# Layer 0 of a four-layer hybrid network: norm and batch statistics moved off VectorE, B replicated in fp32, TensorE's queue reordered

## The chip, the cores and the metric

The kernel runs on one core of one Trainium2 chip, in one launch. The metric is the device time of that core in microseconds. A core has five engines with queues of their own, which the tables below call PE (TensorE), DVE (VectorE), ACT (ScalarE), POOL (GpSimd) and SP (SyncE, which here only starts DMAs). PEld is the loading of TensorE's weights. Each engine takes its instructions in the order in which the program gives them; semaphores make one wait for another.

## The reference, cut to what matters

The input x is 4 images of 96 channels on 64 x 64 points, so 4 sequences of 4096 tokens. Layer 0 is two Mamba blocks, then a 1x1 fusion with a global-pool branch and a batch norm:

```python
mu = seq.mean(-1); var = ((seq - mu) ** 2).mean(-1)
h = (seq - mu) * rsqrt(var + EPS) * ln_g + ln_b          # over the 96 channels
xs, z = split(h @ in_w, 2)
xc = silu(causal conv of 4 taps of xs + conv_b)           # 192 channels
dt, Bm, Cm = split(xc @ xproj_w)                          # 6, 16, 16 columns
delta = softplus(dt @ dt_w + dt_b)
dA = exp(delta * A); dBx = delta * Bm * xc                # 192 x 16 states
hstates[l] = dA[l] * hstates[l-1] + dBx[l]                # along the tokens
y = (sum over states of hstates * Cm + Dp * xc) * silu(z)
seq = seq + y @ out_w                                     # twice (two blocks)
out = fus_w @ [seq, relu(mean(x) @ gp_w)] + fus_b
out = (out - mean) * rsqrt(var + EPS) * bn_g + bn_b + x   # over images and points
```

Layers 1 to 3 (a convolution block, two attention-like blocks with quantised feed-forward parts) come after it, and the change doesn't touch them.

## The kernel before, in words

Layer 0 works through 32 **items** (`items`): 4 stretches s of T = 1024 tokens, times 2 blocks i, times 4 images b. An item has 192 channels x 16 states = 3072 rows, which are 24 **tiles** of 128 rows (32 channels x 4 states) by 1024 tokens. `order` gives the tiles: p picks 64 of the channels, j one half of them, g one of four groups of 4 states. Of the 24 tiles, 8 are "POOL tiles" (`pool_tiles`).

For each tile, `rep` (line 438) spreads 4 rows of B over 128 partitions with a product on PE into PSUM (one replica serves the one or two tiles of a group, nine replicas an item); `exp` (line 447) makes dA on ACT; `scan` (line 464) multiplies delta*xc with the replica on DVE (line 471) and runs the recurrence on DVE (line 475); `times_c` (line 481) multiplies the states with C on POOL; `sum_y` (line 500) sums over states on PE. For a POOL tile the product with B is made on POOL instead (`times_b`, line 461), and ACT writes dA to PSUM (`dap`).

[...] The pool `l0x` holds two buffers of two banks, shared in turn by the replica x, the product u and dap; `l0p` holds two buffers `ps` of one bank, used by every other product; `l0y` holds two for y.

What comes before the tiles of an item is `first_stage` (line 251): load x, centre it, take the norm's scale, multiply, then the products for xc, B, C, dt, delta and z, and the stores of delta and delta*xc to DRAM, from where they are read back spread over partitions. Its steps are hung on **slots** by hand: `at_slot(t)` puts a step beside tile t of the item before. After the tiles come `gate` (line 511, DVE), `project` (line 518) and `finish` (line 527 or 529), the last at slot 17 of the next item, and `keep_stats` (line 537), the batch norm's statistics with `bn_stats` on DVE.

The loop over m at the end of `layer0` sets the order: at each tile it issues the scan, then the next replica (or the exp of the next POOL tile), the exp three tiles ahead, `times_c` of the tile before, then `sum_y` and its like, then the steps hung on this slot. The order is exactly that of the program (`manual_schedule`), so what stands ahead in a queue holds up what is behind it.

In the kernel before, the norm runs so: PE centres (line 274) with the channels on partitions, ACT squares and copies (280, 281), PE sums the squares over channels with a matrix of ones (287), ACT makes the scale as exp(-0.5 ln(.)) (292, 293), DVE multiplies (299). POOL keeps the three last columns for the next stretch (`halo`, lines 268, 301). B is replicated in bf16: ACT casts it three times to bf16, each time what the parts before left over (lines 335, 347), PE subtracts the parts (line 342), and the replica sums the three parts (line 195).

Of the kernel before, what the change touches and what calls it, by code (L numbers as in the profile page):

```python
# [50 lines left out]
class Net:  # L51
# [20 lines left out]
    def consts(self, ctx):  # L72
        tc, nc, ins = self.tc, self.nc, self.ins
        pool = ctx.enter_context(tc.tile_pool(name="const", bufs=1))
        self.cpool = pool
        self.vec = pool.tile([C, NV96], F32, name="vec")
        nc.sync.dma_start(self.vec, ins["vec96"])
        self.vec128 = pool.tile([128, NV128], F32, name="vec128")
        nc.sync.dma_start(self.vec128, ins["vec128"])
        self.ones = pool.tile([C, C], F32, name="ones")  # L80
        nc.vector.memset(self.ones, 1.0)
        self.eps = pool.tile([128, 1], F32, name="eps")
        nc.vector.memset(self.eps, EPS)
        self.ident = pool.tile([128, 128], F32, name="ident")
        make_identity(nc, self.ident)
        self.center = pool.tile([C, C], F32, name="center")
        nc.vector.tensor_scalar_add(self.center, self.ident[:C, :C], -1.0 / C)
        self.stats = pool.tile([C, NT // MB, 6], F32, name="stats")
        self.osc = pool.tile([C, 1], F32, name="osc")
        self.osh = pool.tile([C, 1], F32, name="osh")  # L90


    def layer0(self, dram, scratch):
        tc, nc, ins = self.tc, self.nc, self.ins
        x_in = ins["x"]
        with ExitStack() as ctx:
            cp = ctx.enter_context(tc.tile_pool(name="l0c", bufs=1))
            psum = ctx.enter_context(tc.tile_pool(name="l0p", bufs=2, space=PSUM))
            psum_x = ctx.enter_context(tc.tile_pool(name="l0x", bufs=2, space=PSUM))
# [16 lines left out]
            sel_b = cp.tile([C, 4, 128], BF16, name="sel_bq")  # L116
            part = cp.tile([C, 2, C], BF16, name="partq")
            fo = cp.tile([128, 3, C], F32, name="fo")
            dp = cp.tile([128, 2, 3, 128], F32, name="dp")
            sel_r = load(cp, "sel_r", [128, 32])  # L120
            xproj = load(cp, "xproj", [128, 3, 2, 3 * 2 * NST + DTR])
# [7 lines left out]
            fbias = cp.tile([C, B], F32, name="fbias")  # L129
            pooled = cp.tile([C, B * NSC], F32, name="pooled")  # L130

            with tc.tile_pool(name="l0s", bufs=1) as wk:
# [30 lines left out]
                nc.vector.tensor_copy(sel_b, load(wk, "sel_b", [C, 4, 128]))  # L163
                nc.vector.tensor_copy(part, load(wk, "part", [C, 2, C]))
# [14 lines left out]
            dbl = cp.tile([97 + DTR, T], F32, name="dbl")  # L179
            nc.vector.memset(dbl[C:], 1.0)  # L180
            r3s = [cp.tile([C, T], BF16, name=f"r3{k}") for k in range(2)]
            for r3 in r3s:
                nc.vector.memset(r3, 0.0)
# [7 lines left out]

            def mm(ps, w, rhs, start=True, stop=True, shift=0, **kw):
                for at in halves:
                    at_in = slice(at.start + shift, at.stop + shift)
                    nc.tensor.matmul(ps[:, at], w, rhs[:, at_in], start=start, stop=stop, **kw)  # L195
# [54 lines left out]
            def first_stage(k):  # L250
# [11 lines left out]
                @at_slot(-11)  # L262
                def _():
                    m["xn"] = load_x(b, s, i)
                    if s == 0:
                        nc.gpsimd.memset(n[:, :3], 0.0)
                    else:
                        nc.gpsimd.tensor_copy(n[:, :3], halo[:, b, i])

                @at_slot(-7)  # L270
                def _():
                    m["ps"] = [tile_ps(), tile_ps()]
                    for at, ps in zip(halves, m["ps"]):
                        nc.tensor.matmul(ps, self.center, m["xn"][:, at], start=True, stop=True)

                @at_slot(-6)
                def _():
                    m["sq"] = wk.tile([C, T], F32, name="sq", tag="sq")
                    for at, ps in zip(halves, m["ps"]):
                        nc.scalar.activation(m["sq"][:, at], ps, AF.Square)  # L280
                        nc.scalar.copy(n[:C, 3 + at.start : 3 + at.stop], ps)

                @at_slot(-5)
                def _():
                    m["ps"] = [tile_ps(), tile_ps()]
                    for at, ps in zip(halves, m["ps"]):
                        nc.tensor.matmul(ps, self.ones, m["sq"][:, at], start=True, stop=True)

                @at_slot(-4)
                def _():  # L290
                    for ps in m["ps"]:
                        nc.scalar.activation(ps, ps, AF.Ln, scale=1.0 / C, bias=self.eps[:C])
                        nc.scalar.activation(ps, ps, AF.Exp, scale=-0.5)

                @at_slot(-3)
                def _():
                    for at, ps in zip(halves, m["ps"]):
                        x = n[:C, 3 + at.start : 3 + at.stop]
                        nc.vector.tensor_mul(x, x, ps)  # L299
                    if s < NSC - 1:  # L300
                        nc.gpsimd.tensor_copy(halo[:, b, i], n[:, T:])
# [14 lines left out]
                parts_of("xc", [(w_x[:, i, k], k) for k in range(4)], n, ((-2, 0), (-1, 1), (1, 3)), 2)  # L316

                @at_slot(3)
                def _():
                    nc.scalar.activation(m["xc"], m["xc"], AF.Silu)  # L320
                    exp_set()

                nb = 6 * NST + DTR
                r3 = m["r3"] = r3s[k % 2]

                @at_slot(5)
                def _():
                    m["ps"] = [tile_ps(128), tile_ps(128)]
                    join([ps[:nb] for ps in m["ps"]], xproj[:, :, i], m["xc"])

                @at_slot(6)
                def _():

                    for at, ps in zip(halves, m["ps"]):
                        nc.scalar.copy(r3[:32, at], ps[:32])
                        nc.scalar.copy(dbl[:nb, at], ps[:nb])
                    cd = m["cd"] = dram.tile([2 * NST, T], F32, name="cd", tag="cd", bufs=2)
                    nc.sync.dma_start(cd, dbl[: 2 * NST])

                def less(r):  # L340
                    for at, ps in zip(halves, m["ps"]):
                        nc.tensor.matmul(ps[:C], part[:, r], r3[:, at], start=False, stop=True, skip_group_check=True)

                def next_part(r):
                    rows = slice(32 * r + 32, 32 * r + 64)
                    for at, ps in zip(halves, m["ps"]):
                        nc.scalar.copy(r3[rows, at], ps[rows])

                for r in range(2):
                    at_slot(7 + 2 * r)(lambda r=r: less(r))  # L350
                    at_slot(8 + 2 * r)(lambda r=r: next_part(r))

                parts_of("delta", [(dtw[:, i], 0)], dbl, ((10, 11), (10, 12), (11, 12)), 1)

                @at_slot(12)
                def _():
                    nc.scalar.activation(m["delta"], m["delta"], AF.Softplus)  # L357
                    exp_set()

                parts_of("z", [(w_z[:, i], 3)], n, ((12, 13), (13, 14), (13, 14)), 3)  # L360

                @at_slot(13)
# [18 lines left out]
                @at_slot(19)  # L381
# [56 lines left out]
            def rep(m):  # L438

                k, t = divmod(m, NTL)  # L440
                x = psum_x.tile([128, T], F32, name="rep", tag="xu")
                mm(x, sel_b[:, order[t][1], :], made[k]["r3"])
                u = psum_x.tile([128, T], F32, name="u", tag="xu")
                return x, u

            def exp(m):
# [3 lines left out]
                if on_pool(m):  # L450
                    da = psum_x.tile([128, T], F32, name="dap", tag="xu")
# [11 lines left out]
            def scan(m, x, u):  # L463
# [6 lines left out]
                else:  # L470
                    nc.vector.tensor_mul(u, made[k]["ud", h, j], x)  # L471
# [49 lines left out]
            def finish(k):  # L521
# [3 lines left out]
                for at, ps in zip(halves, made[k]["out"]):  # L525
                    if i == 0:
                        nc.scalar.copy(o[:, at], ps)
                    else:
                        nc.scalar.activation(o[:, at], ps, AF.Identity, bias=fbias[:, b : b + 1])
                a = b * L + s * T  # L530
                nc.sync.dma_start(scratch[:, a : a + T] if i else xd[:, b], o)

            def keep_stats(k):
                b, s, i = items[k]
                a = b * L + s * T
                for at in halves:
                    nc.vector.bn_stats(self.stats[:, (a + at.start) // MB, :], made[k]["x"][:, at])
# [4 lines left out]
            with tc.manual_schedule(engines=engines):  # L542
# [3 lines left out]
                for m in range(first, last + 19):  # L546
                    k, t = divmod(m, NTL)
                    if 0 <= m < last:
                        scan(m, *xu)
                    if 0 <= m + 1 < last:  # L550
                        if on_pool(m + 1):
                            exp(m + 1)
                        elif (t + 1) % NTL in group_starts:
                            xu = rep(m + 1)
# [8 lines left out]
                    for k0 in range(max(k - 1, 0), min(k + 1, len(items))):  # L563
# [15 lines left out]
                        if at == 42 and items[k0][2]:  # L579
                            keep_stats(k0)  # L580
# [8 lines left out]
            nc.vector.bn_aggr(mv, self.stats)  # L589
# [695 lines left out]
def _constants():  # L1285
# [3 lines left out]
    sel_b = np.stack([(k[:, None] % 32 == 4 * g + p[None] // 32) for g in range(4)], 1)  # L1289
    sel_r = (p[:, None] % 32 == p[None, :32]).astype(f32)  # L1290

    part = np.zeros((C, 2, C))
    for r in range(2):
        for q in range(r + 1, 3):
            part[32 * r : 32 * r + 32, r, 32 * q : 32 * q + 32] = -np.eye(32)
# [23 lines left out]
        "part": part.astype(f32),  # L1319
# [102 lines left out]
```

## Time and profile before

The time before is 4220.29 us, the median of three runs (4219.02 to 4225.47). The profiled run took 4222.8 us.

| what | value |
|---|---|
| DVE busy in the whole run | 3189.6 us, 76% |
| POOL busy | 2997.8 us, 71% |
| PE busy | 3233.2 us, 77% |
| ACT busy | 2514.7 us, 60% |
| scans on DVE (L475), all forms | 768, of 2270 to 2348 ns each |
| products with B on DVE (L471) | 512 of 1226 ns |
| products with C on POOL (L481) | 768 of 2359 ns |
| products with B on POOL (L461) | 256 of 2365 ns |
| replicas on PE (L195) | 576 products of 485 ns |

A line of the profile's groups reads: line, engine, operation, what it writes and reads, shapes, count | time busy, mean length of one in ns | idle time of the engine just before them, and what ended that idle time. A line of the timeline gives the start and the length in us, the engine, the line, the operation, the count, and in brackets the idle time before it. One fp32 product shows as two records.

### The profile page before, as it was taken

What the parts mean: (1) busy time and instruction counts of PE and PEld (TensorE: products, weight loads), DVE (VectorE), ACT (ScalarE), POOL (GpSimd) and SP (SyncE); (2) the same over time, 40 slices, a digit from 0 to 9 for tenths busy, and PEclk for the clock granted to TensorE, in tenths of its full rate; (3) what the DMA queues carried; (4) which work ended last, traced back from release to release, by engine and by line L of the source; (5) the groups of instructions that cost most, each with busy time, mean ns of one, the idle gap of its engine ahead of it and who ended that gap; (6) DMA issues with size and microseconds to landing.
All of it is one profiled execution on the core that took longest, in us unless ns stands there. A gap on an engine that the chain in (4) does not pass through costs nothing. (4 is left out here: it accounts for less than half of the span.)

```text
span 4222.8 us, 42511 instructions
## 1 busy us (share of the span) xinstructions
PE 3233.2 (77%) x13088; PEld 1310.8 (31%) x13088; DVE 3189.6 (76%) x2474; ACT 2514.7 (60%) x4098; POOL 2997.8 (71%) x1651
## 2 busy tenths in 40 slices
PE   6677677777767777776777776579999888887987
PEld 2111112111211211121121111277445436555642
DVE  4999999999999999999999999731222583444649
ACT  4666666666666666666666665322555575544547
POOL 1999999999999999999999999611110264333418
PEclk8788888888878888888888887669999998899989
DMA  7557566566656656665665666363000000001111
GB/s 171 136 149 172 132 155 162 139 147 158 164 136 152 161 137 147 161 161 137 151 161 137 147 158 165 77 202 130 0 0 1 1 1 5 23 28 28 44 43 53
DMA packets 183276, 468.02 MB, mean 111 GB/s; under 512 B 53108, under 2 KB 55134, under 8 KB 179968
## 3 DMA queue, kind: packets, MB, share of 16 engines
q1 hardware_dynamic: 183048, 465.31, 43.6%
q8 instruction: 103, 1.69, 0.2%
q14 instruction: 125, 1.02, 0.1%
HBM read 391.62 MB, written 73.50 MB: 110 GB/s over the span
## 5 line engine op out<-in xcount | busy, mean ns | idle before, releaser
L481 POOL TENSOR_TENSOR hs<-hs,crep 128x1024 f32<-128x1024 f32 x768 | 1799.2, 2359 | 108.1 <-DVE hs L475 55.0
L475 DVE TENSOR_TENSOR_SCAN hs<-da,state,u 128x1024 f32<-128x1024 f32 x384 | 901.7, 2348 | 24.9 <-DVE u L471 0.5
L455 ACT ACTIVATE dap<-ddb,nega 128x1024 f32<-128x1024 f32 x256 | 286.3, 1118 | 722.0 <-DVE u L471 721.6
L471 DVE TENSOR_TENSOR u<-udb,rep 128x1024 f32<-128x1024 f32 x512 | 627.7, 1226 | 72.3 <-PE rep L195 40.2
L455 ACT ACTIVATE da<-ddb,nega 128x1024 f32<-128x1024 f32 x512 | 583.7, 1143 | 67.7 <-DVE hs L475 65.7
L195 PE MATMUL rep<-r,sel_bq 96*128 96x512 bf16 x576 | 226.8, 485 | 514.4 <-DVE hs L475 505.9
L461 POOL TENSOR_TENSOR up<-udb,brep 128x1024 f32<-128x1024 f32 x256 | 605.3, 2365 | 4.7 <-DMA ud<-du 4.7
L500 PE MATMUL y<-hs,sel_r 128*32 128x512 f32 x3072 | 501.9, 724 | 4.6 <-POOL hs L481 4.6
L475 DVE TENSOR_TENSOR_SCAN hs<-dap,state,up 128x1024 f32<-128x1024 f32 x192 | 447.1, 2329 | 16.4 <-ACT dap L455 16.4
L205 PE MATMUL ps<-n,w_x 97*64 97x512 f32 x1536 | 424.7, 680 | 10.9 <-DVE n L299 10.8
L475 DVE TENSOR_TENSOR_SCAN hs<-da,u 128x1024 f32<-128x1024 f32 x128 | 293.0, 2289 | 8.1
L195 PEld LDWEIGHTS <-sel_bq 96*128 96x128 bf16 x576 | 39.1, 103 | 780.2 <-DVE hs L475 582.2
L1002 POOL CAST hq<-y 128x512 fp8e5<-128x512 f16 x192 | 118.5, 641 | 222.1 <-DVE y L1001 222.1
L205 PEld LDWEIGHTS ps<-n,w_x 97*64 97x64 f32 x1536 | 152.2, 155 | 287.3 <-issue 217.6
L205 PE MATMUL ps<-n,w_z 97*64 97x512 f32 x384 | 121.1, 714 | 129.3 <-ACT z L309 116.2
L1150 POOL TENSOR_TENSOR av<-av,ec 128x780 f32<-128x780 f32 x32 | 58.8, 1838 | 197.3 <-ACT av L1147 197.3
L796 POOL TENSOR_TENSOR xc<-xc,rs 96x512 f32<-96x512 f32 x32 | 40.4, 1266 | 209.8 <-ACT rs L795 163.8
L500 PEld LDWEIGHTS y<-hs,sel_r 128*32 128x32 f32 x3072 | 65.6, 116 | 319.1 <-issue 167.8
L219 PE MATMUL ps<-xc,xproj 64*102 64x512 f32 x384 | 152.1, 952 | 3.5 <-ACT xc L320 3.5
L475 DVE TENSOR_TENSOR_SCAN hs<-dap,up 128x1024 f32<-128x1024 f32 x64 | 145.3, 2270 | 7.6 <-ACT dap L455 5.7
L373 POOL TENSOR_TENSOR du<-delta,xc 128x512 f32<-128x512 f32 x96 | 122.6, 1277 | 32.1 <-ACT delta L357 22.3
L1147 ACT ACTIVATE av<-xr_ps,vec 128x65 f32<-128x65 f32 x384 | 117.0, 424 | 47.5 <-PE xr_ps L1135 47.5
(255 smaller groups left out, 6067.3 us busy)
## 6 DMA issues: line engine op xcount, KB each, us to landing
ddb<-dd SPq DMA_DIRECT2D x768, 128.0 KB, 3.3
udb<-ud SPq DMA_DIRECT2D x768, 128.0 KB, 4.4
crep<-cd SPq DMA_DIRECT2D x512, 128.0 KB, 4.0
brep<-cd SPq DMA_DIRECT2D x256, 128.0 KB, 3.6
dd<-delta SPq DMA_DIRECT2D x64, 384.0 KB, 3.9
ud<-du SPq DMA_DIRECT2D x192, 128.0 KB, 3.2
band<-in_band SPq DMA_DIRECT2D x24, 1024.0 KB, 4.8
gt<-in_idft SPq DMA_DIRECT2D x64, 256.0 KB, 2.7
```

What stands on the lines that cost most here:

```text
L195: nc.tensor.matmul(ps[:, at], w, rhs[:, at_in], start=start, stop=stop, **kw)
L205: nc.tensor.matmul(ps[rows], w[:, 64 * p : 64 * p + 64], rhs[:, at.start + shift : at.stop + shift], start=k == 0, stop=k == len(ws) - 1, ...
L219: nc.tensor.matmul(ps, w[rows, p], x[rows, p], start=start and p == 0, stop=p == 2)
L373: nc.gpsimd.tensor_mul(u, m["delta"][:, of], m["xc"][:, of])
L455: nc.scalar.activation(da, made[k]["dd", h, j], AF.Exp, scale=nega[:, col : col + 1])
L461: nc.gpsimd.tensor_mul(u, made[k]["ud", h, j], made[k]["brep", g])
L471: nc.vector.tensor_mul(u, made[k]["ud", h, j], x)
L475: nc.vector.tensor_tensor_scan(hs[:, 1:], made[k].pop(("da", t)), u, 0.0 if s == 0 else st, ALU.mult, ALU.add)
L481: nc.gpsimd.tensor_mul(hs[:, :T], hs[:, 1:], made[k]["crep", order[t][1]])
L500: nc.tensor.matmul(made[k]["y", p][row : row + 32], sel_r, made[k]["hs", t][:, at], start=False, stop=True, skip_group_check=True,)
L1002: nc.gpsimd.tensor_copy(q[:, m, :], y2, saturate=False)
L1147: nc.scalar.activation(v[:, k, d], xr[:, at], AF.Identity, scale=self.v128(w, cg + d), bias=self.v128(bias, cg + d))
```

## The change

Four things are done in layer 0:

1. **The norm leaves DVE and goes over tokens on partitions.** PE centres with x as the weights, so that 128 tokens land on partitions and 96 channels lie side by side; ACT squares them and adds up in the same instruction (`accum_out`), makes the scale for 8 x 128 tokens, and multiplies with a scale per partition; PE turns the result back with the identity; ACT copies it to n. The halo copies go from POOL to ACT.
2. **The batch statistics leave DVE.** `finish` adds up its output as it writes it, and a second ACT instruction adds up the squares around a shift (the first half tile's mean).
3. **B is replicated in fp32** straight from dbl, which now has two buffers; the three bf16 parts and their products go. The left half of the tokens is read from rows 0 to 31 and the right half from rows 32 to 63, two copies of B that xproj already makes. The last product with B of a group before a POOL tile is written over its own replica. PSUM's pool has one buffer x, and one that u and dap share, in place of two shared by all three.
4. **PE's steps are moved to other slots**, mostly those behind a replica.

```diff
-            psum_x = ctx.enter_context(tc.tile_pool(name="l0x", bufs=2, space=PSUM))
+            psum_x = ctx.enter_context(tc.tile_pool(name="l0x", bufs=1, space=PSUM))
...
+                @at_slot(-6)
+                    m["ps"] = [tile_ps(128), tile_ps(128)]
+                    for q in range(8):
+                        nc.tensor.matmul(m["ps"][q // 4][:, q % 4 * C : q % 4 * C + C],
+                            m["xn"][:, q * 128 : q * 128 + 128], self.center, start=True, stop=True)
+                @at_slot(-5)
+                    for q in range(8):
+                        nc.scalar.activation(m["nt"][:, q], m["ps"][q // 4][:, q % 4 * C : q % 4 * C + C],
+                            AF.Square, accum_out=m["rs"][:, q : q + 1])
+                    nc.scalar.activation(m["rs"], m["rs"], AF.Ln, scale=1.0 / C, bias=self.eps)
+                    nc.scalar.activation(m["rs"], m["rs"], AF.Exp, scale=-0.5)
+                @at_slot(-4)
+                    for q in range(8):
+                        nc.scalar.mul(m["nt"][:, q], x, m["rs"][:, q : q + 1])
+                @at_slot(-3)
+                    for q in range(8):
+                        nc.tensor.matmul(m["ps"][q // 4][:, q % 4 * 128 : q % 4 * 128 + 128],
+                            m["nt"][:, q], self.ident, start=True, stop=True)
+                @at_slot(-2)
+                        nc.scalar.copy(n[:, :3], halo[:, b, i])
                     for at, ps in zip(halves, m["ps"]):
                         nc.scalar.copy(n[:C, 3 + at.start : 3 + at.stop], ps)
-                        nc.vector.tensor_mul(x, x, ps)
-                        nc.gpsimd.tensor_copy(halo[:, b, i], n[:, T:])
+                        nc.scalar.copy(halo[:, b, i], n[:, T:])
...
-                parts_of("xc", ..., n, ((-2, 0), (-1, 1), (1, 3)), 2)
+                parts_of("xc", ..., n, ((-1, 1), (0, 2), (2, 4)), 2)
-                @at_slot(5)
+                @at_slot(7)
                     join([ps[:nb] for ps in m["ps"]], xproj[:, :, i], m["xc"])
-                        nc.scalar.copy(r3[:32, at], ps[:32])
                         nc.scalar.copy(dbl[:nb, at], ps[:nb])
-                for r in range(2):
-                    at_slot(7 + 2 * r)(lambda r=r: less(r))
-                    at_slot(8 + 2 * r)(lambda r=r: next_part(r))
-                parts_of("delta", ..., ((10, 11), (10, 12), (11, 12)), 1)
+                parts_of("delta", ..., ((9, 10), (9, 10), (10, 11)), 1)
-                parts_of("z", ..., ((12, 13), (13, 14), (13, 14)), 3)
+                parts_of("z", ..., ((11, 12), (12, 13), (13, 14)), 3)
...
-                x = psum_x.tile([128, T], F32, name="rep", tag="xu")
-                mm(x, sel_b[:, order[t][1], :], made[k]["r3"])
-                u = psum_x.tile([128, T], F32, name="u", tag="xu")
+                x = psum_x.tile([128, T], F32, name="rep", tag="x")
+                for q, at in enumerate(halves):
+                    rows = slice(32 * q, 32 * q + 32)
+                    nc.tensor.matmul(x[:, at], sel_b[rows, order[t][1]], made[k]["dbl"][rows, at], start=True, stop=True)
...
+                    u = x if on_pool(m + 1) else psum_x.tile([128, T], F32, name="u", tag="u")
                     nc.vector.tensor_mul(u, made[k]["ud", h, j], x)
...
-                        nc.scalar.activation(o[:, at], ps, AF.Identity, bias=fbias[:, b : b + 1])
+                    nc.scalar.activation(o[:, at], ps, AF.Identity, bias=fbias[:, b : b + 1], accum_out=self.sums[:, a : a + 1])
+                    nc.scalar.activation(ps, ps, AF.Square, bias=sbias[:, b : b + 1], accum_out=self.squares[:, a : a + 1])
-                    nc.vector.bn_stats(self.stats[:, (a + at.start) // MB, :], made[k]["x"][:, at])
```

## The prediction

> **What bounds the kernel now.** I read the page's slices first: VectorE (DVE) and GpSimd (POOL) stand at 9 tenths from slice 2 to slice 26, so layer 0 is where the change acts; the chain of work that ended last shows only later layers. Then the stretches, 500 us each, inside that plateau (columns after the length: PE, PEld, DVE, ACT, POOL busy, granted clock, DMA share, GB/s):
>
> ```profile
> 500.00:1000.00 500.00, 363.96 (x1432) 95.02 (x1428) 476.43 (x283) 334.52 (x515) 476.85 (x226) 0.83 0.62 151
> 1000.00:1500.00 500.00, 363.00 (x1402) 96.00 (x1404) 479.39 (x285) 329.13 (x510) 477.19 (x226) 0.82 0.60 149
> ```
>
> Two engines are busy 95%, and each feeds the other. ACT (66%) and PE (73%) matter only where one of the two waits for them. Next, the groups by shape in 500 to 2500 us:
>
> ```profile
> L481 POOL TENSOR_TENSOR hs<-hs,crep 128x1024 f32<-128x1024 f32 x586 | 1372.4, 2358 | 80.3 <-DVE hs L475 38.0 <-DMA udb<-ud 19.3 <-DMA crep<-cd 10.4
> L475 DVE TENSOR_TENSOR_SCAN hs<-da,state,u 128x1024 f32<-128x1024 f32 x343 | 805.4, 2348 | 22.3 <-DVE u L471 0.5
> L471 DVE TENSOR_TENSOR u<-udb,rep 128x1024 f32<-128x1024 f32 x391 | 479.4, 1226 | 48.0 <-PE rep L195 26.0 <-DMA ud<-du 3.7
> L475 DVE TENSOR_TENSOR_SCAN hs<-dap,state,up 128x1024 f32<-128x1024 f32 x172 | 400.5, 2329 | 15.2 <-ACT dap L455 15.2
> ...
> L299 DVE TENSOR_TENSOR n<-n,ps 96x512 f32<-96x512 f32 x48 | 31.1, 668 | 0.3
> ...
> L537 DVE BATCH_NORM_STATS2 stats<-x 96x6 f32<-96x512 f32 x24 | 15.1, 668 | 0.0
> ...
> L268 POOL COPY n<-halo 97x3 f32<-97x3 f32 x23 | 4.4, 192 | 0.0
> L301 POOL COPY halo<-n 97x3 f32<-97x3 f32 x17 | 3.2, 188 | 14.2 <-DVE n L299 14.2
> ```
>
> The 586 times-C products are 24 per item: 24.4 items in 2000 us, a period of **81.9 us per item**, and 32 items make layer 0. The four stretches from 500 to 2500 sum to 1908.6 us of DVE and 1905.7 of POOL: 78.2 and 78.0 of a period. Of DVE's 3.7 idle us, named waits are 26.0 (replica), 15.2 (dap) and 3.7 us of 2000: 1.8 an item. The other 1.9 are the steps between instructions. POOL idles 3.9, of which 14.2/24.4 = 0.6 is the halo copy waiting for the norm.
>
> Last the timeline of one item, PE alone but for one DVE line (start, length, instructions):
>
> ```profile
> 1004.47 1.03 PE L195 MATMUL rep<-r,sel_bq 96*128 96x512 bf16 x2 [6.49 <-DVE hs L475]
> ...
> 1026.44 1.12 PE L492 MATMUL y<-xc,dp 128*128 128x512 f32 x2
> ...
> 1035.81 1.32 PE L205 MATMUL ps<-n,w_z 97*64 97x512 f32 x4 [3.68 <-ACT z L309]
> ...
> 1038.92 1.03 PE L195 MATMUL rep<-r,sel_bq 96*128 96x512 bf16 x2
> ...
> 1039.99 1.23 DVE L471 TENSOR_TENSOR u<-udb,rep 128x1024 f32<-128x1024 f32 x1 [0.76 <-PE rep L195]
> ...
> 1041.66 2.82 PE L219 MATMUL ps<-z,out_w 64*96 64x512 f32 x12
> ```
>
> A replica is released when the scan before a POOL tile ends, and has that tile's scan (2.33 us) to hide in. It does so unless PE comes late: at 1038.92 it stood behind the z product, which had waited for ACT's copy.
>
> [...] after 6.49 us idle a replica takes 1.03 us, others 0.60. [...] 12 records of z,out_w (two sets of 64 rows) took 2.82 us, 0.43 for each pair; a lone fp32 product needs 0.43 per record (dp: two records in 1.12). No run yet shows sets of 32 rows. [...]
>
> **The change part by part.**
>
> *DVE loses* two norm products (31.1/24.4 = 1.27 us an item) and bn_stats (15.1/24.4 = 0.62): **1.9 us**, all of it in the queue of a 95% engine. It gains one-off small operations only.
>
> *POOL loses* both halo copies, 7.6/24.4 = 0.3, and the 0.6 of waiting behind one: 0.9. A wait for PE's reads remains only for the memset of the first 8 items.
>
> *Replica in fp32.* Nine per item, two products of 32 rows each. If the row sets run together: two steps of 0.43 plus the tail that dp shows (1.12 - 0.86 = 0.26) = 1.12 us warm against 0.60; at half clock two of 0.85 plus about 0.3 = 2.0 against 1.03. Window: 1004.47 to the next product's start at 1006.76 is 2.29. Both fit, the cold one by 0.3. If they run one after the other: 1.98 warm, 3.7 cold; the cold one misses by 1.4. I take together, since the trace shows it for 64 rows at 96 columns, and keep the other for the range. The product over its own replica (line 473 of the changed kernel) costs nothing: DVE still reads and writes PSUM; and dap's own buffer is free after the scan of the tile before last, not after the last product, which can only help the 15.2 us of dap waits.
>
> *TensorE's order.* In the changed program's queue z stands two slots ahead of the replica of slot 15 (one before), xproj stands behind that of slot 7, center behind that of slot 18. The 26.0/24.4 = 1.07 us of replica waits came mainly from two lateness spots per item (0.76 at 1039.99, 0.63 at 1050.19), one behind z and one behind center: both orders are cured. I credit 0.8.
>
> *B without its three bf16 parts.* Four small PE products (4 x 0.38) and six ACT casts (6 x 0.57 = 3.4) go; dbl gets a second buffer. All of it lay beside the scans, so I count nothing; delta comes a slot earlier and its store with it.
>
> *Norm on ACT and PE.* ACT loses squares, copies, Ln, Exp (2 x (0.60 + 0.58 + 0.64 + 0.57) = 4.8) and the 3.4 of casts. It gains 8 squares with a sum, Ln and Exp of 8 columns, 8 scalings, 2 copies (1.16), the halo copies (0.36), and 0.7 for half the items' second batch sum. An ACT copy of 97x96 took 0.24 us (L936); how much a sum adds the trace doesn't show: nothing, or at most a second instruction of 0.24. So the eight squares take 1.9 to 3.9, I take 2.6; the scalings 2.0. Sum 2.6 + 0.5 + 2.0 + 1.2 + 0.4 + 0.7 = 7.4 against 8.2: ACT stays near 66%. But order counts: ACT's exp for the POOL tile of slot 21 is queued behind the squares, and these wait for center. From the replica of slot 18: replica 1.1, y 1.06, eight transposing products at 0.43 (L714, of like shape: 55.2 us busy, 128 products) 3.4, the last four squares and Ln, Exp 1.8, exp 1.1 = 8.5 us; DVE needs it after a POOL scan and two tiles, 2.33 + 2 x 3.6 = 9.5. Hidden by 1; cold PE takes 1 to 3 us more. I charge 0.4 an item.
>
> *POOL nearer its limit:* at 80 us it would idle 2.3, where waits for DMA (29.7/24.4 = 1.2) remain. I charge 0.3 for the coupling.
>
> *Ends:* the first item's norm is longer by some 4 us at half clock, its B parts shorter by 3; the small operations at the end replace bn_aggr (1.0). Nothing.
>
> Sum per item: -1.9 - 0.8 + 0.4 + 0.3 = -2.0; times 32 = -64; **4220 - 64 = 4156 us**.
>
> **The rivals.**
> (a) *Small gain:* POOL is as loaded as DVE, and once DVE is ahead only POOL's 0.9 counts: 32 x 0.9 = 29, 4191. For it: 78.0 against 78.2. Against: much of POOL's idle time (38.0) is waiting for DVE, which a faster DVE shortens.
> (b) *A new wait eats it:* the ACT block or cold replicas hold DVE for 2 us an item, 4220 or a little more; 4222.
> (c) *Row sets in series:* in the timeline of one item four of nine replicas take 1.03 us, so are cold: 4 x 1.4 = 5.6, the warm ones that come late add 1, less 2.7: +3.9 an item, 4345. For it: no set of 32 rows at 128 columns is in the trace. Against: pairs of 64 rows at 102 columns (xproj) do go together.
>
> **How the numbers follow.** Forecast 0.56, (a) 0.20, (b) 0.13, (c) 0.11. If DVE's named waits vanish too, the period is 78.2 + 1.9 - 1.9 = 78.2: -3.7 x 32 = 4102; half-way, 4125, is the low end. The high end takes in (a) and (b): 4228. Outside stay most of (c) and a tail below, 0.14. Faster by over 0.2% (below 4212): 0.56 + 0.20 + a little of (b) = 0.78; same 0.06; slower 0.16.
>
> **What would show it.** Right: period near 80 us; no norm product or bn_stats on DVE; waits of DVE for the replica under 26 us in 2000, replicas of 1.1 (warm) and 2.0 us (cold); POOL over 96% busy. Wrong: replica records that follow each other at 0.43 steps four times; DVE waiting for dap at slot 21 in every item; squares of over 0.5 us; POOL waiting for DMA for 2 us an item, which would leave the period at 81.

## The result and the profile after

The changed kernel takes **4105.66 us** (median of four runs, 4099.68 to 4110.68) against 4222.64 for the kernel before on the same chip: ratio 0.9723, 95% interval [0.9706, 0.974], 117 us faster. The forecast was 4156, with 4125 as its low end: right in direction, too small by almost half.

Read on the two profiled runs (4222.8 and 4106.5 us), the 116.3 us lie here. The scans, from the first one's start to the last one's end, take 2516.2 us in place of 2615.8 (-99.6). The first scan starts at 81.8 in place of 91.1 (-9.3). From the last scan to the batch norm's reciprocal it is 14.7 in place of 16.4 (-1.8). Layers 1 to 3, in which no instruction changed, are 5.6 us shorter; over the 14 profiles of this study that stretch varies from 1488.5 to 1499.4, so this part says nothing.

The stretches of the changed kernel inside layer 0 (columns as before: PE, PEld, DVE, ACT, POOL, clock, DMA share, GB/s):

```profile
1000.00:1500.00 500.00, 412.76 (x1728) 129.63 (x1728) 486.06 (x276) 339.51 (x675) 496.09 (x224) 0.83 0.67 160
1500.00:2000.00 500.00, 410.98 (x1726) 126.32 (x1722) 485.68 (x274) 334.25 (x635) 494.99 (x223) 0.83 0.64 154
```

POOL is now busy 99%, DVE 97%, in place of 95% each. The groups by shape in 500 to 2500 us:

```profile
L484 POOL TENSOR_TENSOR hs<-hs,crep 128x1024 f32<-128x1024 f32 x610 | 1426.2, 2360 | 23.7 <-DVE hs L478 18.5 <-ACT rs L283 1.3 <-PE ps L296 1.2
...
L478 DVE TENSOR_TENSOR_SCAN hs<-da,state,rep 128x1024 f32<-128x1024 f32 x183 | 429.7, 2348 | 15.9
L478 DVE TENSOR_TENSOR_SCAN hs<-dap,state,up 128x1024 f32<-128x1024 f32 x183 | 426.1, 2329 | 5.7 <-ACT dap L456 5.5
...
L442 PE MATMUL rep<-dbl,sel_b 32*128 32x512 f32 x914 | 321.4, 779 | 360.0 <-DVE hs L478 345.1 <-DVE u L474 13.4 <-PE y L503 0.9
...
L474 DVE TENSOR_TENSOR u<-udb,rep 128x1024 f32<-128x1024 f32 x202 | 248.3, 1229 | 26.0 <-PE rep L442 8.7
L474 DVE TENSOR_TENSOR rep<-udb,rep 128x1024 f32<-128x1024 f32 x204 | 247.6, 1214 | 0.3
```

610 products with C are 25.4 items in 2000 us, so 78.7 us an item in place of 81.9. No instruction has become faster: scans still take 2348 and 2329 ns, products 2360. What went is DVE's own extra work and its waits: replica 26.0 to 8.7 us, dap 15.2 to 5.5, POOL's wait for the scan 38.0 to 18.5.

The norm and the POOL tile behind it, in the timeline of one item:

```profile
1007.93 1.13 PE L442 MATMUL rep<-dbl,sel_b 32*128 32x512 f32 x4 [1.12 <-DVE hs L478]
...
1009.99 2.02 PE L264 MATMUL ps<-center,x 96*128 96x96 f32 x16
...
1011.15 0.25 ACT L277 ACTIVATE nt<-ps 128x96 f32<-128x96 f32 x1 [2.46 <-PE ps L264]
1011.30 0.19 ACT L277 ACTIVATION_READ_ACCUMULATOR nt<-ps 128x1 f32 x1
...
1013.78 1.12 ACT L456 ACTIVATE dap<-ddb,nega 128x1024 f32<-128x1024 f32 x1
...
1015.95 1.95 ACT L290 ACTIVATE nt<-ps,rs 128x96 f32<-128x96 f32 x8
...
1017.83 2.33 DVE L478 TENSOR_TENSOR_SCAN hs<-dap,state,up 128x1024 f32<-128x1024 f32 x1
1018.06 2.08 PE L442 MATMUL rep<-dbl,sel_b 32*128 32x512 f32 x4 [4.16 <-DVE hs L478]
```

From the replica to the end of dap's exp it takes 14.90 - 7.93 = 7.0 us, and DVE asks for it after 9.9: in this item the centring and the squares are hidden with 2.9 us to spare. The two replica lines are warm and cold: 1.13 us at a granted clock of 1.00, 2.08 us at 0.50.

### The profile page after: what moved, and what is told of

It reads as the page before. It is cut to its first block, busy times and chain, and to the rows that moved or that the text cites. A ratio compares the mean times of both kernels' runs of the same rounds, so it can differ in the third digit from the quotient of the medians.

```text
span 4106.5 us, 45550 instructions
## 1 busy us (share of the span) xinstructions
PE 3374.3 (82%) x14304; PEld 1459.6 (36%) x14304; DVE 3125.3 (76%) x2382; ACT 2474.1 (60%) x4690; POOL 2988.3 (73%) x1603
## 3 DMA queue, kind: packets, MB, share of 16 engines
q1 hardware_dynamic: 182904, 465.17, 45.6%
## 5 line engine op out<-in xcount | busy, mean ns | idle before, releaser
L442 PE MATMUL rep<-dbl,sel_b 32*128 32x512 f32 x1152 | 405.4, 780 | 465.7 <-DVE hs L478 439.4
L478 DVE TENSOR_TENSOR_SCAN hs<-da,state,rep 128x1024 f32<-128x1024 f32 x192 | 450.8, 2348 | 16.7
L478 DVE TENSOR_TENSOR_SCAN hs<-da,state,u 128x1024 f32<-128x1024 f32 x192 | 450.9, 2348 | 10.1
L442 PEld LDWEIGHTS rep<-dbl,sel_b 32*128 32x128 f32 x1152 | 108.7, 217 | 758.9 <-issue 513.7
L198 PE MATMUL ps<-n,w_x 97*64 97x512 f32 x1536 | 366.3, 620 | 4.4 <-POOL n L307 4.2
L474 DVE TENSOR_TENSOR u<-udb,rep 128x1024 f32<-128x1024 f32 x256 | 314.7, 1229 | 65.3 <-PE rep L442 43.9
L474 DVE TENSOR_TENSOR rep<-udb,rep 128x1024 f32<-128x1024 f32 x256 | 310.7, 1214 | 0.4
L198 PEld LDWEIGHTS ps<-n,w_x 97*64 97x64 f32 x1536 | 108.2, 140 | 253.4 <-issue 202.4
L346 ACT COPY dbl<-ps 102x512 f32<-102x512 f32 x64 | 34.3, 588 | 199.7 <-PE ps L212 199.7
L478 DVE TENSOR_TENSOR_SCAN hs<-da,rep 128x1024 f32<-128x1024 f32 x64 | 146.5, 2289 | 5.4
```

The costliest lines, as they stand in the source:

```text
L198: nc.tensor.matmul(ps[rows], w[:, 64 * p : 64 * p + 64], rhs[:, at.start + shift : at.stop + shift], start=k == 0, stop=k == len(ws) - 1, ...
L442: nc.tensor.matmul(x[:, at], sel_b[rows, order[t][1]], made[k]["dbl"][rows, at], start=True, stop=True)
L478: nc.vector.tensor_tensor_scan(hs[:, 1:], made[k].pop(("da", t)), u, 0.0 if s == 0 else st, ALU.mult, ALU.add)
```

## The experiments

Each kernel was timed beside the kernel before on the same chip. For each I read, from its profile, the length of the scans and what DVE and POOL do per item (mean of items 5 to 28). Busy is the time in which at least one instruction runs, so two that overlap count once.

| kernel | ratio to before [95%] | first scan at | scans take | DVE busy + idle an item | POOL idle an item |
|---|---|---|---|---|---|
| before | 1 | 91.1 | 2615.8 | 78.16 + 3.83 | 3.86 |
| changed | 0.9723 [0.9706, 0.974] | 81.8 | 2516.2 | 76.33 + 2.46 | 0.89 |
| e1 before + order | 1.0021 [1.0014, 1.0028] | 87.3 | 2631.8 | 78.32 + 4.18 | 4.41 |
| e9 before + order + PSUM | 0.9899 [0.9881, 0.9917] | 88.3 | 2580.5 | 77.74 + 3.13 | 2.78 |
| e10 before + norm, halo, statistics | 1.0136 [1.0121, 1.015] | 93.3 | 2673.8 | 76.82 + 7.38 | 6.22 |
| e11 e9 and e10 together | 0.9742 [0.9725, 0.9758] | 88.1 | 2516.0 | 76.29 + 2.55 | 0.95 |
| e2 changed, order undone | 0.9929 [0.9914, 0.9944] | 82.3 | 2588.6 | 76.21 + 5.01 | 3.26 |
| e3 changed, PSUM undone | 0.9775 [0.976, 0.9789] | 82.5 | 2531.0 | 76.65 + 2.61 | 1.43 |
| e4 changed, statistics undone | 0.9742 [0.9729, 0.9755] | 82.6 | 2518.6 | 76.47 + 2.34 | 0.96 |
| e5 changed, two gates twice | 0.9842 [0.9828, 0.9855] | 83.6 | 2561.8 | 77.60 + 2.57 | 2.27 |
| e6 changed, halo on POOL | 0.9724 [0.971, 0.9737] | 82.4 | 2513.7 | 76.47 + 2.29 | 0.59 |
| e7 changed, replica in series | 1.0163 [1.0142, 1.0184] | 83.2 | 2689.7 | 76.19 + 7.85 | 5.96 |
| e8 changed, shifted bias on ACT | 0.9709 [0.9696, 0.9723] | 83.1 | 2506.9 | 76.00 + 2.46 | 0.57 |
| e12 changed, shifted bias by columns | 0.971 [0.9696, 0.9724] | 83.0 | 2507.2 | 76.01 + 2.37 | 0.55 |

**e1: the order alone, on the kernel before:** two moves, of the centring product and of softplus, that clear the replica's two late spots.

```diff
-                @at_slot(-7)        # centring product
+                @at_slot(-6)
-                @at_slot(12)        # softplus of delta, ahead of z's parts
+                @at_slot(13)        # softplus of delta, behind the copy of z's first part
```

> The kernel before with two moves alone: the centring product goes one slot later, behind the replica of slot 18, and the softplus block on ACT stands behind the copy of z's first part, so that z's last product no longer waits before the replica of slot 15. Theory A (TensorE's order held DVE, and that wait counted in full): DVE's wait for the replica falls from 26 us in 2000 to about 8, that is 0.7 us an item, 4220 - 23 = 4197. Theory B (POOL, busy 78.0 of 81.9 us, sets the period, and a wait of DVE is slack): under 5 us, 4215 to 4220.

Measured 1.0021: neither, it is 9 us slower. Its waits in 500 to 2500 us (who waited for whom: us in total, times, longest):

```profile
...
DVE hs L475 <- ACT dap L455: 40.1, 46, 2.2
POOL halo L301 <- DVE n L299: 26.2, 17, 2.6
DVE n L299 <- ACT ps L293: 10.7, 23, 0.5
...
DVE u L471 <- PE rep L195: 0.5, 1, 0.5
```

The wait for the replica went from 26.0 to 0.5 us, just as it should. But dap's rose from 16.2 to 40.1, the halo's from 14.2 to 26.2, and the norm's products now waited too: one wait was turned into three.

**e9: the same, with dap in another buffer than the replica, and the last product of a group over its replica.**

```diff
-  x, u and dap: two buffers, tag "xu"
+  x: one buffer, tag "x";  u and dap: one buffer, tag "u"
+  u = x if on_pool(m + 1) else psum_x.tile([128, T], F32, name="u", tag="u")
```

> The kernel before with the two moves of the first experiment (centring product and softplus block) and with the changed kernel's PSUM (dap has a buffer of its own with u, the last product of a group goes over its replica). Alone, the two moves cleared the wait for the replica (26 to 0.5 us in 2000) but raised that for dap (16 to 40) and gained nothing. Theory A (dap's shared buffer was what stood in the way): the wait for dap falls under 15, the period by 1 us an item or more, ratio 0.990 to 0.993. Theory B (dap waits because ACT itself is late, behind the squares): no gain, 0.998 to 1.002.

Measured 0.9899, and the waits say a part of why:

```profile
...
DVE hs L475 <- ACT dap L454: 19.9, 29, 1.3
...
DVE n L299 <- ACT ps L293: 10.7, 23, 0.5
```

dap's wait fell from 40.1 to 19.9, about 0.8 us an item, and that for the replica stayed away. The other part shows in when products start. Those of tiles 1, 6, 9, 14 and 17 go over their replica and follow a scan directly. In e1, where the buffer that they write is by the program the one that this scan reads, they start 0.03 (1, 9, 17) or 0.10 us (6, 14) after its end; here they start 0.08 us before its end (medians). Over the five that is 0.7 us an item. The two parts make about 1.5 of the (2631.8 - 2580.5)/32 = 1.6 us an item between e1 and e9.

Theory A's gain is there, but only about half of it is dap's, and dap waits more than the 15 us I had set. Order and PSUM together are worth 43 us by the ratio, and the order alone nothing. PSUM alone was not run on the kernel before, so what it does there without the order isn't known.

**e10: the work taken off DVE, and nothing else.** The norm block, the halo copies and the statistics of the changed kernel stand in the kernel before, the norm one slot earlier so that it ends where the old one did.

```diff
+  centre at -7, squares at -6, scaling at -5, turning back at -4, copies and halo at -3 (all as in the changed kernel)
+  sums and squares on ACT in finish, no bn_stats
```

> The kernel before with the norm, the halo copies and the batch statistics as in the changed kernel, and with B, the order of TensorE (but for the norm's own steps) and PSUM as they were. Theory A (the DVE time taken away counts in full, waits stay): 1.8 us an item, 58 us, less 8 for the one slow instruction: ratio 0.988. Theory B (the waits for the replica grow, since center and its squares still stand ahead of the replica of slot 18): 0.992 to 1.0. Theory C (the waits fall by themselves with the halo's): 0.980 or less.

Measured 1.0136, slower by more than any of the three: DVE has 1.3 us less to do an item and 3.6 us more to wait.

```profile
...
DVE u L492 <- PE rep L198: 59.4, 42, 3.8
DVE hs L496 <- ACT dap L476: 52.6, 47, 1.7
```

Most of the new wait for the replica is at one spot, the product of tile 19, whose replica is issued at slot 18. The centring product (L273, slot 17) stands ahead of that replica and needs the two `ps` buffers. `finish` holds these until ACT has also made the squares of the batch statistics (L558):

```profile
2000.99 1.13 PE L273 MATMUL ps<-center,x 96*128 96x96 f32 x8 [3.21 <-ACT ps L558]
...
2001.51 0.64 ACT L558 ACTIVATE ps<-ps,sbias 96x512 f32<-96x512 f32 x1
...
2002.33 2.02 PE L273 MATMUL ps<-center,x 96*128 96x96 f32 x8 [0.20 <-ACT ps L558]
...
2004.14 1.06 PE L198 MATMUL rep<-r,sel_bq 96*128 96x512 bf16 x2
...
2005.24 1.23 DVE L492 TENSOR_TENSOR u<-udb,rep 128x1024 f32<-128x1024 f32 x1 [3.31 <-PE rep L198]
```

Beside a `finish` with these sums that product waits 2.0 to 3.8 us, beside one without them 0.6 to 1.0; in the kernel before it waits 0.6 or less, once 1.3 (items 5 to 28).

**e11: e9 and e10 together**, so all of the change but B in fp32 and the slots that come with it.

> The two before put together, with the norm at the changed kernel's slots: all of the change but B in fp32 and the slots that it makes possible. If B in fp32 brings nothing of its own (the forecast's reading): ratio 0.972 to 0.976. If the shorter B part and its order are part of the gain: 0.978 to 0.988.

Measured 0.9742; the scans take 2516.0 us, to 0.2 the changed kernel's. So B in fp32, with its slots, brings nothing to the period. It brings the start: first scan at 88.1 here, 81.8 there. The work taken off DVE makes the kernel 1.36% slower on the old order and buffers, and takes the ratio from 0.9899 to 0.9742 on the new ones, where the centring product stands behind the replica of slot 18.

**e2: the changed kernel with the old slots** of delta, softplus, z and centring.

```diff
-                @at_slot(-6)
+                @at_slot(-7)
-   delta ((9, 10), (9, 10), (10, 11)), softplus 11, store 12, z ((11, 12), (12, 13), (13, 14))
+   delta ((10, 11), (10, 12), (11, 12)), softplus 12, store 13, z ((12, 13), (13, 14), (13, 14))
```

> The changed kernel with the slots of delta, softplus, z and the centring product put back where they were before. Theory A (TensorE's order is part of the gain): waits for the replica come back at two spots of an item, 0.7 us an item, of which DVE's slack of some 0.6 us hides a part: 4110 to 4128. Theory B (POOL sets the period at 78.5 us whatever DVE waits for): 4106 within 5.

Measured 0.9929: 87 us of the 117 are gone, far over both.

```profile
DVE u L474 <- PE rep L442: 88.0, 54, 4.5
```

The waits do come back at two spots, the products of tiles 16 and 19, but the second is larger than it was. Before these two products DVE idles, in us an item (items 5 to 28):

| kernel | tile 16 | tile 19 |
|---|---|---|
| before | 0.97 | 0.32 |
| e10 | 1.15 | 1.93 |
| e2 | 1.10 | 1.97 |
| changed | 0.09 | 0.25 |

e10 has the same waits with bf16 replicas, so it isn't the replica in fp32 that makes them. At tile 19 the centring product stands ahead of the replica again and waits for the sums on ACT, as in e10. The old slot did little harm to the old norm and much to the new one.

**e3: the changed kernel with the old PSUM.**

```diff
-  name="l0x", bufs=1;  tags "x" and "u"
+  name="l0x", bufs=2;  one tag "xu", u from its own buffer
```

> The changed kernel with PSUM as before: two buffers that the replica, the product u and dap share in turn, and no product over its own replica. Theory A (dap's own buffer took away part of DVE's waits): DVE's wait for dap comes back, 0.4 us an item, 4110 to 4119. Theory B (only TensorE's order and the removed work count): 4106 within 5.

Measured 0.9775, 22 us slower than the changed kernel by the ratio and 14.8 us in the scans: theory A's direction. Its reason fails: DVE's wait for dap is 0.2 us here. What grew is seen in the starts, as in e9: the products of tiles 1, 6, 9, 14 and 17, which no longer go over their replica, start 0.03 to 0.10 us after the scan ahead of them ends in place of, mostly, 0.08 before. That is 0.7 us an item; some 0.2 come back in smaller waits for dap, and the period grew by 0.5. The instructions are as long as before: DVE's busy time rose (76.33 to 76.65) because they overlap less.

**e5: more work for DVE.** After the first two gate products of an item the same product is done once more.

```diff
                 nc.vector.tensor_mul(z, made[k]["y", p], z)
+                if p < 2:
+                    nc.vector.tensor_mul(junk, made[k]["y", p], z)
```

> The changed kernel with two of the three gate products of an item done twice on DVE, the second into a tile that nobody reads: 2 x 0.67 = 1.3 us more for DVE an item, about what the norm's products took, behind no new wait. Theory A (DVE sets the period): all of it, 32 x 1.3 = 43 us, ratio 0.982 to the kernel before. Theory B (POOL sets it and DVE has 0.6 us of slack): 0.7 us an item, 23 us, 0.978. Theory C (DVE is far from the limit): 0.972 as without it.

Measured 0.9842. DVE got 1.27 us more to do an item, and the scans took 45.6 us longer, 1.4 an item. All of it counts: DVE sets the period.

**e6: more work for POOL.**

```diff
-                        nc.scalar.copy(n[:, :3], halo[:, b, i])       # slot -2
+                        nc.gpsimd.tensor_copy(n[:, :3], halo[:, b, i])  # slot -11
-                        nc.scalar.copy(halo[:, b, i], n[:, T:])       # slot -2
+                        nc.gpsimd.tensor_copy(halo[:, b, i], n[:, T:])  # slot -1
```

> The changed kernel with the halo copies back on POOL, at slots where what they wait for is done early: 0.3 to 0.4 us more for POOL an item. Theory B (POOL sets the period): 0.3 to 0.4 us an item, 10 to 13 us, ratio 0.975. Theory A (DVE sets it): nothing, 0.972.

Measured 0.9724, no difference, with POOL's busy time up by 0.28 us an item and its idle time down to 0.59. POOL is nearly full and still not the one that sets the period. It has little room left, though: the 0.6 us that it idles here and in e8 are, as an estimate from these traces, about the most that less work on DVE could still bring.

**e4: statistics back on DVE** (bn_stats after finish, bn_aggr at the end, no sums on ACT).

```diff
-  nc.scalar.activation(o[:, at], ps, AF.Identity, bias=..., accum_out=...); nc.scalar.activation(ps, ps, AF.Square, ...)
+  nc.scalar.activation(o[:, at], ps, AF.Identity, bias=...)
+  nc.vector.bn_stats(self.stats[:, (a + at.start) // MB, :], made[k]["x"][:, at])    # at 42
```

> The changed kernel with the batch statistics back on DVE (bn_stats, bn_aggr), without the sums and squares on ACT. It gives DVE 0.62 us an item. Theory B (POOL sets the period, DVE has some 0.6 us of slack an item): nothing from that, and the 8 us that DVE spends in the one instruction that makes the shifted bias are saved: 4097 to 4101. Theory A (DVE sets the period): +20 - 8 = 4118.

Measured 0.9742 [0.9729, 0.9755], which overlaps the changed kernel's interval: moving the statistics is worth nothing that this measurement can tell. The forecast of theory A, 4118 or a ratio of 0.975, lies in the interval; that of theory B, 0.971, lies outside. Against e8, which is free of the slow instruction as well, the scans are 11.7 us longer, 0.37 an item with DVE's busy time up 0.47. So the work counted; the instruction described next paid it back.

**e8 and e12: one instruction of 7.8 us.** In the changed kernel the shifted bias of the squares, 96x4 values, is made once on DVE. DVE's and POOL's timelines there:

```profile
529.05 0.15 DVE L538 TENSOR_SCALAR shift<-sums 96x1 f32<-96x1 f32 x1 [0.68 <-ACT x L534]
529.24 7.79 DVE L539 TENSOR_SCALAR sbias<-fbias,shift 96x4 f32<-96x4 f32 x1
536.94 2.28 DVE L478 TENSOR_TENSOR_SCAN hs<-dap,up 128x1024 f32<-128x1024 f32 x1
```

```profile
531.16 1.25 POOL L370 TENSOR_TENSOR du<-delta,xc 128x512 f32<-128x512 f32 x1
532.38 2.32 POOL L484 TENSOR_TENSOR hs<-hs,crep 128x1024 f32<-128x1024 f32 x1
534.67 2.33 POOL L462 TENSOR_TENSOR up<-udb,brep 128x1024 f32<-128x1024 f32 x1
539.39 2.35 POOL L484 TENSOR_TENSOR hs<-hs,crep 128x1024 f32<-128x1024 f32 x1 [2.39 <-DVE hs L478]
```

It starts while POOL works without a break and ends at 537.03, when POOL has just run out of work (537.00). Seven of the other kernels have the same instruction. In e2, e3, e5, e6, e10 and e11 it took 4.9 to 10.8 us and ended within 0.03 us of the end of POOL's last instruction before a pause; in e7 it took 0.65 us and ended 0.02 us after a POOL product, though POOL went on at once. Why it got through there isn't known.

```diff
-  nc.vector.tensor_scalar(sbias, fbias, self.shift, None, ALU.subtract)
+  nc.scalar.activation(sbias, fbias, AF.Identity, bias=self.shift)          # e8, shift with the sign turned
+  nc.vector.tensor_scalar(sbias[:, c : c + 1], fbias[:, c : c + 1], self.shift, None, ALU.subtract)   # e12, four times
```

> The changed kernel with the shifted bias of the batch statistics (96x4 values, once in the whole run) made on ACT in place of DVE. In the trace of the changed kernel this one DVE instruction lasts 7.8 us and its item 87.0 us in place of 78.5. If the instruction itself is what holds DVE (it starts while POOL computes and ends when POOL runs out of work): the item falls to about 78.5 and the time by 8 us, ratio 0.970. Rival (the item would lose the time to another wait, on ACT's sum): 0.972.

> The changed kernel with the one slow DVE instruction (shifted bias, 96x4 values) split into four of one column each. If it was slow because it [...] had to wait for POOL: one column needs no such thing, as the instruction before it (96x1, 0.15 us) shows; four of 0.15 to 0.2 us, and its item falls from 87.0 to about 79: ratio 0.970. If any DVE instruction at that place waits for POOL: several us again, 0.972.

Measured 0.9709 and 0.971; the item falls from 87.0 to 79.2 and 80.3 us, the scans from 2516.2 to 2506.9 and 2507.2. In e12 DVE does the same subtraction in four instructions:

```profile
L540 DVE TENSOR_SCALAR sbias<-fbias,shift 96x1 f32<-96x1 f32 x4 | 0.6, 203 | 0.0
```

203 ns each beside a POOL no less busy (idle 0.55 us an item, 0.89 in the changed kernel). Both kernels have lower medians (4100.97 and 4098.33) than the changed one and better ratios, though the intervals overlap; the 9 us are read from the scans.

**e7: both halves of a replica from the same rows.**

```diff
-                    rows = slice(32 * q, 32 * q + 32)
+                    rows = slice(0, 32)
```

> The changed kernel with both halves of a replica taken from rows 0 to 31, so that its two products share the same rows of the array. If products run together only when their rows differ (theory of the prediction): a replica takes 1.98 us warm and 3.7 cold in place of 1.13 and 2.08, cold ones miss the POOL tile's scan by 1.4 us, four an item: 5 us an item, 160 us more, ratio 1.01. Rival (they run together anyway, or the window has room): 0.972 to 0.976.

Measured 1.0163. The replica lines of e7:

```profile
1029.89 3.75 PE L442 MATMUL rep<-dbl,sel_b 32*128 32x512 f32 x4 [1.93 <-DVE hs L478]
1042.04 1.98 PE L442 MATMUL rep<-dbl,sel_b 32*128 32x512 f32 x4
```

1.98 us warm and 3.75 cold where the changed kernel has 1.13 and 2.08. The times fit products of 32 rows at 128 columns that run together when they read different sets of rows, and one after the other when they read the same set. Reading different sets is worth 4.4% here.

## Why the prediction was right or wrong

**Right: what comes off DVE.** The forecast took 1.9 us an item; DVE's busy time fell by 1.83. In that stands one of the "one-off small operations", the slow instruction, with 7.79/24 = 0.32 us an item; without it busy time fell by 2.15 (e12). That DVE's work counts in full is shown by e5 for the finished kernel. But e10 shows a condition that the forecast didn't have: on the old order and buffers the same removal makes the kernel slower, since the norm's products, its squares and the batch sums lengthen the waits for replica and dap by more than they spare. That the norm went to ACT and not to POOL was my choice; of that block only the halo copies were also run on POOL (e6), so no run says what the rest would have done there.

**Right: the replica in fp32.** Estimated 1.12 us warm and 2.0 cold, measured 1.13 and 2.08; in series 1.98 and 3.7 estimated, 1.98 and 3.75 measured. The cold figures were estimates from the kernel before, where the granted clock was 0.50 in the replica of 1.03 us (at 1004.47) and 1.00 in one of 0.60 us (at 1030.52). Its pairs of 64 rows show in the times as well: 12 records of z,out_w took 2.82 us at 1.00, and 12 of xproj 4.68 us at 0.60 on average (1005.43 to 1010.11), where 12 in series would take 5.2 even at 1.00: an estimate at 0.43 a record, which is (1.98 - 1.12)/2 from the four records of a replica in e7 and the two of dp. Rival (c) is out, and its price was 4345 against the 4289 of e7.

**Wrong: the terms "- 0.8 + 0.4 + 0.3".** This is the step that failed. They come to 0.1 us an item less between DVE's instructions. In the traces (items 5 to 28) the time between them fell from 2.41 to 0.96 us, by 1.45; the instructions themselves sum to 1.75 less.

- The 0.8 for TensorE's order was about right: DVE's wait for the replica fell from 26.0/24.4 to 8.7/25.4, by 0.7.
- The PSUM edit was put at nothing ("costs nothing", "can only help"). The products over their own replica start earlier by 0.7 in all, as in e9 and e3, and dap's wait fell from 15.2/24.4 to 5.5/25.4, by 0.4.
- The charges, 0.4 for the ACT block and 0.3 for POOL, didn't come.

These make 1.8; some 0.3 of it is lost again, because the norm's products and the statistics had themselves started before the instruction ahead of them ended.

The runs give the same size by another way: order and PSUM spare (2615.8 - 2580.5)/32 = 1.1 us an item on the old kernel (e9), and on top of that the work taken off DVE, with the norm at its new slots, spares (2580.5 - 2516.0)/32 = 2.0 (e11). Together that is 3.1 where the forecast had 2.0; times 32 it is the 99.6 us of the scans. This split holds for this path only: with the work taken off first (e10) the scans are 1.8 us an item longer, and order, PSUM and the later slots then spare 4.9. The parts can't be priced one by one and added. The order does nothing for the old kernel without PSUM (e1); the changed kernel without PSUM is only 14.8 us of scans behind (e3).

Why the two charges didn't come, the trace shows. From the replica to the end of dap's exp I had 8.5 us, and it took 7.0. The eight centring products I priced at 3.4 us from a like shape (L714), and they took 2.02 at a granted clock of 1.00; those of L714 lie in a stretch (2731 to 2786 us of the kernel before) where the granted clock was 0.50. The squares took 2.0 with their sums, not 2.6. The 1 to 3 us that a cold PE was to add were a guess of mine that no trace had shown. So 2.9 us are spare in the item shown, not 1. The coupling with POOL: e6 shows that POOL takes 0.28 us an item more without loss, at 0.59 us idle. The forecast's low case, in which all named waits vanish (period 78.2, 4102 us), came near in time, but waits of 0.6 us an item are left, and 9.3 us came from the start. I cut the range half-way to it, on the thought that some wait always stays.

**Wrong: "Ends: nothing".** The first scan starts 9.3 us earlier. I weighed the longer norm of the first item, 4 us, against its shorter B parts, 3 us, both estimates. With the new norm on the old order the first scan starts 2.2 us later (e10), and B's shorter chain, with its slots, brings 6.3 (from e11 to the changed kernel). What I left out is what stands ahead of the first replica. Before:

```profile
82.07 7.17 PE L205 MATMUL ps<-n,w_x 97*64 97x512 f32 x16 [4.24 <-DVE n L299]
...
89.17 0.61 PE L195 MATMUL rep<-r,sel_bq 96*128 96x512 bf16 x2
```

After:

```profile
79.11 1.13 PE L442 MATMUL rep<-dbl,sel_b 32*128 32x512 f32 x4
...
80.17 4.23 PE L198 MATMUL ps<-n,w_x 97*64 97x512 f32 x18
```

The second item's xc products stood ahead of the first replica, at a granted clock of 0.61 on average (7.17 us for 16 records; in the lines after, 18 take 4.23 at 1.00), and now stand behind it. With B's old chain the first scan still waits until 88.1 (e11), for a DMA of delta*xc. That the moved products alone bring the 3 us from 91.1 to 88.1 isn't shown: e1, where they still stand ahead of the replica, starts at 87.3.

**The rivals.** (a), that only POOL's 0.9 us would count, is refuted by the result and by e5 and e6. (b), a new wait that eats the gain, didn't happen here, but it is what e1, e2 and e10 show, each with parts of the change left out. In e2 and e10 much of it comes from the sums on ACT, which hold up TensorE and through it DVE.

## What to carry to other kernels

When two in-order engines are both nearly full, as here, a wait that is removed can give way to another that would have ended just after it (e1): size the waits together, and test an order and the buffers that it needs both as one edit and each alone. A product that may write elsewhere than the instruction ahead of it reads can start sooner, here by 0.7 us an item over five products, which no list of waits shows (e9, e3). Work moved to idle engines is not free by their idle share; it is free if nothing on the full engine waits behind it, which is a matter of what stands ahead of what (e10: 1.3 us an item less for DVE to do, 3.6 more to wait). And where the named waits of a full engine all have a cure in the change, the case in which they all vanish deserves a chance of its own and the range must reach it.

## What the runs showed of the hardware that was not expected

A small DVE instruction was slow beside POOL: 96x4 fp32 values from SBUF to SBUF took 7786 ns while POOL worked without a break, and four of 96x1 took 203 ns each (e12). In all eight kernels that have it, it ended within 0.03 us of the end of a POOL instruction; in seven of them it took 4.9 to 10.8 us, in e7 0.65. What in the larger instruction made it slow isn't shown: e12 has 1 column in place of 4, and no other shape was run. The large DVE products and scans, which each read one operand from PSUM, show no such delay beside the same POOL (the scans of one form, `hs<-da,state,u`, take 2348 ns before and after the change and in e7, the products 1226 and 1229 ns before and after). To read SBUF alone isn't enough for the delay: `bn_stats` of 96x512 reads no PSUM and took 668 ns in the kernel before, two of them 1.26 us beside a POOL product of 2.37 (at 557.97).

A sum along an ACT instruction shows as a second one, ACTIVATION_READ_ACCUMULATOR, of 193 to 220 ns on average, which mostly overlaps its neighbours. Eight squares of 128x96 with their sums take 2.0 us, and so do the eight scalings of the same shape without sums (1.95). At 96x512 the next ACT instruction starts 0.67 us after one with a sum (L534 of the changed kernel) and 0.58 us after one without (L529 of the kernel before): 0.09 us for the sum.
